# A planner that orders five queues: durations fitted to the trace, and a planned wait of VectorE for GpSimd

## The chip, the core and the metric

The kernel runs on one core of one Trainium2 chip. The metric is the device time of one execution in microseconds (us). Three executions of the kernel before took 3527.23, 3532.02 and 3536.44 us, so the median is 3532.02 us.

A core has engines that work side by side, each through its own queue and strictly in the order of that queue: TensorE (PE in the profile, its weight loads PEld), VectorE (DVE), ScalarE (ACT), GpSimd (POOL) and SyncE (SP), which here issues all DMAs. SBUF is the memory on the chip, PSUM the memory in eight banks that matmuls write. DVE and ACT read PSUM; POOL works on SBUF alone.

## What is computed

Two layers over 128 sequences of 32 tokens and 256 features. Each layer attends to a context of 257 tokens for every sequence, then does self-attention, then a feed-forward block; in the second layer the attention to the context is joined by a gated second attention, and the feed-forward block is eight experts with a router.

```python
x = x + _L0_xattn_ref(_layernorm(x), ctx_2048, ...)        # 16 heads, keys with an RMS norm
x = x + _L0_attn_ref(_layernorm(x), ...)                   # differential attention
x = x + _L0_ffn_ref(_layernorm(x), ...)                    # weights through a 4-bit round trip
x = x + _L1_xattn_ref(_layernorm(x), mask, ctx_2048, ...)  # 32 heads, rotary, gate
x = x + _L1_attn_ref(_layernorm(x), ...)                   # 16 heads, causal
x = x + _L1_ffn_ref(_layernorm(x), ...)                    # 8 experts, top-2 fallback
return x
```

## The kernel before

**Tiling.** Four sequences of 32 tokens make one tile of 128 rows (`h`, 32 tiles). Values are kept as a 16-bit high part and a 16-bit remainder, so that fp32 accuracy comes out of 16-bit matmuls. Nearly every PSUM result therefore is read twice: ACT writes the high part, DVE subtracts it from PSUM and writes the remainder (`split_ps`, lines 381 to 388). For softmax weights ACT writes the exponential `P` and POOL the remainder `Pl` (`expP`, lines 918 to 925).

**Streams.** The work is written as some 30 streams, each a generator: loading and projecting the context (`ctx`), `rowpass` (row maxima of the scores, tiles `mx`, `m16`, `pl`, `mT`), `pvpass` (exponentials and the products with V, tiles `P`, `Pl`, `Uc`), the layer norm `ln_T` (tiles `bmv`, `brs`, `lnh`) ahead of every block, the self-attentions B and E, the feed-forward blocks C and F, and so on. The first layer's streams run until about 1,770 us of the trace, the second layer's after that; streams of one layer overlap freely.

**The planner.** Class `Est` (lines 87 to 223) decides the order. Each instruction is emitted through a wrapper (`Eng`, line 226, with its call in line 234, which is why every line of the profile says L234), and `Est.note` gives it a planned start: not before its operands are there, and then in the first gap of its engine that is long enough (`fit`, line 111), so that a later emitted instruction can be planned into an earlier gap. How long it holds its engine comes from `Est.cost` (line 137), a table of formulas in nanoseconds by engine, operation, element count and place of the operands. `LAT` (line 90) is added until a consumer on another engine may start.

The plan is used twice. `pipeline` (line 355) picks the stream that goes on next by the planned time at which it can. At the end the instructions of each of the five queues PE, ACT, DVE, POOL and DMA are sorted by planned start, and a dependence from each to the next pins that order into the program (lines 376 to 379):

```python
for L in [est.log[k] for k in PIN]:
    L.sort(key=lambda x: x[:2])
    for (_, _, a), (_, _, b) in zip(L, L[1:]):
        self.tc.add_manual_dep(b, a.name, dep, reason="issue order")
```

Planned times never reach the chip: an instruction starts there when its queue comes to it and its semaphores allow. Only the order is the plan's.

Of the kernel before, what the change touches and what calls it, by code (L numbers as in the profile page):

```python
# [17 lines left out]
PSUM = bass.MemoryType.PSUM  # L18
# [66 lines left out]


class Est:
    """Estimates when each instruction can run. It only decides the order in which units of work are emitted."""

    LAT = {"pe": 196.0, "act": 150.0, "dve": 135.0, "pool": 75.0, "dma": 910.0}  # L90

    def __init__(self):
        self.busy = {k: ([], []) for k in ("pe", "act", "dve", "pool", "hw", "dma")}
        self.w, self.r, self.free, self.slots, self.rec = {}, {}, {}, {}, []
        self.end = self.pe = 0.0
        self.cols, self.acc, self.prev, self.first, self.group = {}, {}, {}, {}, {}
        self.log = {k: [] for k in ("pe", "act", "dve", "pool", "dma")}

# [37 lines left out]
    @staticmethod  # L136
    def cost(e, op, outs, ins):
        def n(a):
            return math.prod(a.shape[1:])

        def half(a):
            return mybir.dt.size(a.dtype) == 2 and a.space != PSUM
        o = outs[0]
        if e == "pe":
            if op == "transpose":
                return max(25.0, n(o) / 2.4 * (2 if mybir.dt.size(ins[0].dtype) == 4 else 1))
            return 426.0 if mybir.dt.size(ins[0].dtype) == 4 else max(25.0, n(ins[1]) / 2.4 + 1.0)
        m = max([n(o)] + [n(a) for a in ins])
        if e == "act":
            return (50.0 if ins[0].space == PSUM else 92.0) + 93.0 * (len(ins) > 1) + 0.84 * m  # L150
        if e == "pool":
            return 300.0 + 165.0 * n(o) if n(o) <= 8 else 149.0 + 2.1 * m
        f = 1.0
        if op == "transpose":
            return 602.0
        if all(half(a) for a in [o] + [a for a in ins if n(a) > 1]):
            f = 0.5 if op == "tensor_tensor" else 0.3
        return 68.0 + 1.04 * m * f

    @staticmethod  # L160
    def region(a):
# [17 lines left out]
    def note(self, e, op, outs, ins, inst):  # L179
        t = 0.0  # L180
        R = [(a.tensor.name, self.region(a)) for a in ins]
        Wr = [(a.tensor.name, self.region(a)) for a in outs]
        for w, L in ((False, R), (True, Wr)):
            for n, (p0, p1, lo, hi) in L:
                t = max(t, self.first.get(n, 0.0), self.group.get(n, 0.0) if e == "pe" else 0.0)
                if w:
                    t = max(t, self.free.get(n, 0.0))
                    if n not in self.first:
                        t = max(t, self.first.get(self.prev.get(n), 0.0) + 1.0)
                for (q0, q1, l2, h2, wr), (end, by) in self.acc.get(n, {}).items():  # L190
                    if (w or wr or h2 == PSB) and q0 < p1 and p0 < q1 and l2 < hi and lo < h2:
                        t = max(t, end if (w or h2 == PSB) and by == e and e != "dma" else end + self.LAT[by])
        if e == "dma":
            t = self.fit("hw", t, 500.0)
            st = t - 500.0
            end = self.fit("dma", t + 650.0, math.prod(outs[0].shape) * mybir.dt.size(outs[0].dtype) / 360.0)
        else:
            d = self.cost(e, op, outs, ins)
            if e == "pe" and self.cols.get(int(t / TICK) - 1, 0.0) < WARM:
                d = max(25.0, 2.0 * d - 1.0)  # L200
            end = self.fit(e, t, d)
            st = end - d
            if e == "pe":
                k = int(end / TICK)
                self.cols[k] = self.cols.get(k, 0.0) + math.prod(ins[-1].shape[1:]) * ins[0].shape[0] / 128
                self.pe = max(self.pe, end)
                self.group[Wr[0][0]] = end
        self.log[e].append((st, len(self.log[e]), inst))
        for n, _ in Wr:
            self.first.setdefault(n, st)  # L210
        fin, end = end, end + self.LAT[e]
        for n, k in R:
            A = self.acc.setdefault(n, {})
            k += (False,)
            A[k] = max(A.get(k, (0.0, e)), (fin, e))
            self.r[n] = max(self.r.get(n, 0.0), end)
        for n, (p0, p1, lo, hi) in Wr:
            A = self.acc.setdefault(n, {})
            for k in [k for k in A if p0 <= k[0] and k[1] <= p1 and lo <= k[2] and k[3] <= hi]:
                del A[k]  # L220
            A[p0, p1, lo, hi, True] = (fin, e)
            self.w[n] = max(self.w.get(n, 0.0), end)
        self.end = max(self.end, end)
# [1449 lines left out]
```

## Time and profile before

| | value |
|---|---|
| median of 3 runs | 3532.02 us (3527.23 to 3536.44) |
| profiled execution, first to last instruction | 3532.9 us |
| mean granted TensorE clock | 0.917 of full speed |
| instructions | 95,750 |
| DVE / ACT / POOL instructions | 7,365 / 6,339 / 2,313 |
| HBM traffic | 318.82 MB read, 180.19 MB written, 141 GB/s |

Busy time in two long stretches, one in each layer (us, and share of the stretch):

| stretch | PE | DVE | ACT | POOL | PE clock |
|---|---|---|---|---|---|
| 353 to 1590 (1237 us) | 1104.6 (89%) | 975.5 (79%) | 807.6 (65%) | 821.8 (66%) | 0.97 |
| 1943 to 3356 (1413 us) | 1224.6 (87%) | 1209.4 (86%) | 956.6 (68%) | 782.2 (55%) | 0.90 |

How to read it: the span lies within the spread of the timed runs, so sums made on the trace can be set against the median as they are. A group of instructions is given by engine, operation, what it writes and reads, its shapes, its count, its busy time and the mean of one in ns. The recorded length of an instruction is not quite the time that it holds its engine: on DVE the next instruction often starts some 80 ns before the record of the last ends, on ACT some 100 ns, on POOL some 40 ns.

### The profile page before, as it was taken

The numbers are of one execution on the slowest core, as the hardware profiler recorded it, in microseconds if no ns is written. First come the engines' busy times: TensorE is split into PE (matmuls) and PEld (weight loads), VectorE is DVE, ScalarE is ACT, GpSimd is POOL, SyncE is SP. The second block draws the span as 40 slices with busy tenths as digits, with TensorE's granted clock in tenths as the row PEclk, the third lists the DMA queues.
The fourth block names the chain that finished last, engine by engine and source line by source line (L and its number), as shares of the span: only waits on it lengthen the run. The fifth ranks groups of instructions, "written<-read, shape, count | busy, mean of one in ns | idle before, by whom it ended". The sixth has DMA issues, their size and how long they took to land.

```text
span 3532.9 us, 95750 instructions
## 1 busy us (share of the span) xinstructions
PE 3027.0 (86%) x35473; PEld 2261.8 (64%) x35473; DVE 2868.5 (81%) x7365; ACT 2239.1 (63%) x6339; POOL 2020.9 (57%) x2313
## 2 busy tenths in 40 slices
PE   5889898898888899898776889989888898888888
PEld 2545666666666666665564677767676776766676
DVE  6888787788777887878777888879888888898876
ACT  3446666566666676675567766676676775766672
POOL 2445666666666676675564554555555655555562
PEclk9989999999999999998876899989898998989999
DMA  5646676666677677676546434454454544445420
GB/s 138 194 142 194 178 203 191 188 182 193 195 207 209 193 209 214 180 209 187 129 117 175 109 88 91 113 112 95 105 120 101 119 111 94 99 104 117 107 50 10
DMA packets 685970, 509.90 MB, mean 144 GB/s; under 512 B 226524, under 2 KB 673244, under 8 KB 685500
## 3 DMA queue, kind: packets, MB, share of 16 engines
q1 hardware_dynamic: 685500, 503.77, 54.2%
q8 instruction: 279, 4.57, 0.6%
q14 instruction: 191, 1.56, 0.2%
HBM read 318.82 MB, written 180.19 MB: 141 GB/s over the span
## 4 chain that ended last, share of the span: by engine, by line
DVE 18%; PE 16%; ACT 8%; DMA 5%; issue 2%; SPq 1%; POOL 1%; DVEq 0%; ACTq 0%; POOLq 0%
PE bank L234 16%; DVE mx L234 4%; DMA QstD<-ed 2%; ACT P L234 1%; ACT Uc L234 1%; DVE dS L234 1%; DVE xt L234 1%; SPq L234 1%; DVE eS L234 1%; DVE glu_t L234 1%; DVE fhid L234 1%; DVE lnh L234 1%; DVE rbt L234 1%; ACT Qb L234 1%; DVE s L234 1%
## 5 line engine op out<-in xcount | busy, mean ns | idle before, releaser
L234 POOL TENSOR_TENSOR Pl<-P 128x512 f16<-128x512 f32 x768 | 813.6, 1075 | 317.7 <-ACT P L234 313.5
L234 ACT ACTIVATE P<-bank 128x512 f32<-128x512 f32 x768 | 438.4, 600 | 114.8 <-PE bank L234 94.3
L234 DVE TENSOR_REDUCE mx<-bank 128x2 f32<-128x512 f32 x768 | 479.6, 681 | 7.9 <-PE bank L234 7.9
L234 ACT COPY Uc<-bank 32x68 f32<-32x68 f32 x1536 | 314.7, 205 | 159.9 <-PE bank L234 142.2
L234 ACT CAST vv<-bank 128x256 f16<-128x256 f32 x512 | 200.9, 403 | 251.5 <-DVE vv L234 119.6
L234 PE MATMUL bank<-V,P 128*128 128x68 f16 (+1 forms) x4096 | 304.6, 199 | 26.9 <-ACT P L234 16.6
L234 DVE TENSOR_TENSOR vv<-bank,vv 128x256 f16<-128x256 f32 x512 | 213.1, 423 | 122.9 <-ACT vv L234 115.3
L234 POOL TENSOR_TENSOR fhl<-fhid 128x256 f16<-128x256 f32 x256 | 156.7, 615 | 273.0 <-DVE fhid L234 229.6
L234 PE MATMUL bank<-V,Pl 128*128 128x36 f16 (+1 forms) x3072 | 290.7, 194 | 10.7 <-POOL Pl L234 10.6
L234 PEld LDWEIGHTS <-P 128*128 128x128 bf16 x4096 | 264.8, 102 | 42.4 <-issue 16.7
L234 PEld LDWEIGHTS <-Kst 97*128 97x128 f16 x4096 | 240.5, 102 | 76.2 <-issue 48.2
L234 PEld LDWEIGHTS <-Pl 128*128 128x128 f16 x3072 | 243.7, 100 | 41.9 <-POOL Pl L234 17.4
L234 ACT ACTIVATE glu_t<-bank 128x256 f32<-128x256 f32 x352 | 134.1, 383 | 172.3 <-PE bank L234 138.3
L234 PE MATMUL bank<-QstD,Kst 97*128 97x128 f16 x2048 | 207.0, 233 | 29.6 <-ACT P L234 9.5
L234 PEld LDWEIGHTS <-ch 128*128 128x128 f16 x2048 | 196.3, 100 | 54.8 <-issue 23.4
L234 POOL TENSOR_TENSOR kk<-kb,kk 128x512 f16<-128x512 f32 x128 | 147.1, 1167 | 111.0 <-ACT kk L234 110.8
L234 PEld LDWEIGHTS <-hT 128*128 128x128 f16 x1536 | 138.0, 103 | 113.3 <-issue 34.7
L234 PE MATMUL bank<-khf,eh 32*128 32x256 f16 (+1 forms) x1536 | 153.8, 296 | 56.8 <-DMA khf<-kd 13.7
L234 DVE SCALAR_TENSOR_TENSOR glu_t<-glu_t,bank 128x256 f32<-128x256 f32 x352 | 144.8, 411 | 68.6 <-ACT glu_t L234 67.3
L234 POOL TENSOR_TENSOR cl<-ct,ch 128x1024 f16<-128x1024 f32 x64 | 137.5, 2149 | 34.6 <-DMA xt<-in_x 22.5
L234 POOL TENSOR_TENSOR ss<-ss,sq 128x512 f32<-128x512 f32 (+1 forms) x65 | 82.7, 1272 | 120.9 <-ACT sq L234 72.9
L234 POOL TENSOR_TENSOR rbt<-rbt,rbt 128x512 f32<-128x512 f32 x64 | 83.0, 1297 | 100.9 <-DVE rbt L234 72.1
(470 smaller groups left out, 9459.5 us busy)
## 6 DMA issues: line engine op xcount, KB each, us to landing
Kst<-kd SPq DMA_DIRECT2D x384, 256.0 KB
kd<-kk SPq DMA_DIRECT2D x128, 512.0 KB
vd<-vv SPq DMA_DIRECT2D x256, 136.0 KB
V<-vd SPq DMA_DIRECT2D x64, 544.0 KB
vd<-vv SPq DMA_DIRECT2D x256, 132.0 KB
V<-vd SPq DMA_DIRECT2D x64, 528.0 KB
ct<-in_ctxm SPq DMA_DIRECT2D x64, 512.0 KB
khf<-kd SPq DMA_DIRECT2D x128, 256.0 KB
```

The lines of the kernel that those rows point to most:

```text
L234: r = f(*a, **k)
```

## The change

Only `Est` is touched: no instruction is added or taken away, and no operand, tile or buffer changes. Three things are done.

First, `cost` is rewritten for ACT, POOL and some of DVE. Second, a new function `lock` moves the planned ready time of a DVE instruction to the end of the POOL operation that is planned to run at that moment, if it is a `tensor_scalar`, `tensor_copy`, `tensor_tensor` or `scalar_tensor_tensor` and none of its operands lies in PSUM. Third, `note` keeps the planned spans of POOL in a list `pl` for that purpose.

```diff
         if e == "act":
-            return (50.0 if ins[0].space == PSUM else 92.0) + 93.0 * (len(ins) > 1) + 0.84 * m
+            ps = ins[0].space == PSUM
+            d = (50.0 if ps else 92.0) + (127.0 if ps else 93.0) * (len(ins) > 1) + 0.84 * m
+            return d + 100.0 * (len(outs) > 1) + 112.0 * (o.shape[0] in (32, 64))
         if e == "pool":
-            return 300.0 + 165.0 * n(o) if n(o) <= 8 else 149.0 + 2.1 * m
+            if n(o) <= 8:
+                return 350.0 + 160.0 * n(o)
+            d16 = mybir.dt.size(o.dtype) == 2
+            k = (1.665 if mybir.dt.size(ins[-1].dtype) == 2 and ins[-1].tensor.name == ins[0].tensor.name else 1.9) if d16 else 2.1
+            if any(a.ap[-1][0] == 0 for a in ins):
+                k = 1.68
+            return 147.0 + k * m
         f = 1.0
         if op == "transpose":
             return 602.0
         if all(half(a) for a in [o] + [a for a in ins if n(a) > 1]):
             f = 0.5 if op == "tensor_tensor" else 0.3
-        return 68.0 + 1.04 * m * f
+        if op == "reciprocal":
+            f = 5.0
+        d = 58.0 * (op == "scalar_tensor_tensor" and len(ins) > 2)
+        if op == "tensor_copy" and ins[0].space == PSUM and o.shape[0] < 32:
+            f = 0.5
+        return 68.0 + d + 1.04 * m * f
+
+    def lock(self, t, op, outs, ins):
+        if not self.pl or any(a.space == PSUM for a in outs + ins) or op not in ("tensor_scalar", "tensor_copy", "tensor_tensor", "scalar_tensor_tensor"):
+            return t
+        i = bisect.bisect_right(self.pl, (t, 1e18)) - 1
+        return max(t, self.pl[i][1]) if i >= 0 else t
...
             d = self.cost(e, op, outs, ins)
             if e == "pe" and self.cols.get(int(t / TICK) - 1, 0.0) < WARM:
                 d = max(25.0, 2.0 * d - 1.0)
+            if e == "dve":
+                t = self.lock(t, op, outs, ins)
             end = self.fit(e, t, d)
             st = end - d
+            if e == "pool":
+                bisect.insort(self.pl, (st, end))
+                if len(self.pl) > 4000:
+                    del self.pl[:1000]
```

`m` is the largest element count per row among the operands, `n(o)` that of the output, `o.shape[0]` the number of rows written; `len(ins) > 1` is true for an ACT instruction with a scale or bias column, `len(outs) > 1` for one that also writes a row sum.

More of the change, by code (lines that the diff above doesn't have):

```diff
@@ L95, in __init__ @@
         self.end = self.pe = 0.0
+        self.pl = []
         self.cols, self.acc, self.prev, self.first, self.group = {}, {}, {}, {}, {}
```

## The prediction

> **What bounds the kernel now.** I read the page from the top: busy time, then the slices, then the chain of waits.
>
> ```profile
> PE 3027.0 (86%) x35473; PEld 2261.8 (64%) x35473; DVE 2868.5 (81%) x7365; ACT 2239.1 (63%) x6339; POOL 2020.9 (57%) x2313
> ...
> DVE 18%; PE 16%; ACT 8%; DMA 5%; issue 2%; SPq 1%; POOL 1%; DVEq 0%; ACTq 0%; POOLq 0%
> ```
>
> No engine is full. The reader is to see that PE and DVE are both near 85%, and that the chain (it could be followed through the last 51% of the span) lies on DVE for 18 of its 51 points, on PE for 16, on ACT for 8. The order of the queues decides, and DVE is the engine that is last most often: a us saved on DVE is worth about 18/51 = 0.35 us at the end. I use that factor below; it is a choice, since shares of a chain are not a derivative.
>
> Next I asked whether the DVE's busy time is work. The timeline of DVE over 900 to 912 us:
>
> ```profile
> 903.07 0.16 DVE L234 TENSOR_TENSOR mx<-mx,pl 128x8 f32<-128x8 f32 x1
> 903.31 0.43 DVE L234 TENSOR_TENSOR vv<-bank,vv 128x256 f16<-128x256 f32 x1
> 903.65 0.67 DVE L234 TENSOR_SCALAR m<-mx 128x8 f16<-128x8 f32 x1
> ...
> 909.35 0.15 DVE L234 TENSOR_SCALAR brs<-bmv 128x1 f32<-128x1 f32 x1
> ...
> 910.37 0.70 DVE L234 TENSOR_SCALAR bsm<-bsm,nlam 128x2 f32<-128x2 f32 x1
> ```
>
> and of POOL over the same time:
>
> ```profile
> 902.03 2.27 POOL L234 TENSOR_TENSOR kk<-kb,kk 128x512 f16<-128x512 f32 x2 [4.28 <-ACT kk L234]
> ...
> 908.66 1.27 POOL L234 TENSOR_TENSOR ss<-ss,sq 128x512 f32<-128x512 f32 x1 [2.10 <-ACT sq L234]
> 910.01 1.04 POOL L234 TENSOR_TENSOR sl<-ss 128x512 f16<-128x512 f32 x1
> ```
>
> An eight-element instruction takes 0.67 us and ends at 904.32, POOL's pair ends at 904.30; a two-element one takes 0.70 us and ends at 911.07, POOL's `sl` at 911.05. `vv`, with an operand in PSUM (`bank`), runs through the same POOL work in its usual 0.43. So DVE instructions without a PSUM operand do wait on the chip for POOL, inside their own record. The one-element `brs` does not: 0.15 us in the middle of `ss`.
>
> **How much that wait is.** Groups with shapes kept apart, mean of one in ns, against the median of the same tile's instructions (which is unwaited, as most of a group doesn't wait):
>
> ```profile
> L234 DVE TENSOR_SCALAR lnh<-xt,bmv,brs 128x256 f32<-128x256 f32 x192 | 123.6, 659 | 8.7 <-POOL brs L234 6.9 <-PE bank L234 1.1
> L234 DVE TENSOR_SCALAR eh<-qT,const 128x256 f16<-128x256 f16 x128 | 68.3, 590 | 0.0
> L234 DVE TENSOR_SCALAR m<-mx 128x8 f16<-128x8 f32 x64 | 24.8, 387 | 0.8
> L234 DVE TENSOR_SCALAR brs<-bmv 128x1 f32<-128x1 f32 x128 | 19.1, 150 | 2.7
> ```
>
> `lnh`: 192 x (659 - 414) = 47 us. `eh`: 128 x (590 - 279) = 40. The six narrow groups of the row pass (`mx`, `m`, `pl` at 8 and 16 elements, 64 each; means 400, 348, 387, 374, 372, 291, medians 173, 173, 169): 73. `eS`: 128 x (439 - 285) = 20. `nfmk`: 180 x (395 - 290) = 19. `bS`: 64 x (373 - 280) + 64 x (452 - 352) = 12. `e`: 64 x (463 - 343) = 8. Sum 219; the other narrow groups (`bss`, `bmx`, `aos`, `bsm`, `qn`, the router's) bring some 80. **About 300 us of DVE's 2868 is waiting for POOL**, by the single records in 521 instructions of some 2,120 of this kind, 0.57 us each. By stretch, 132 us lie in 353 to 1590 and 100 us in 1943 to 3356. The plan before knows nothing of it.
>
> **The change, part by part.**
>
> *The planned wait.* The chip waits already; new is only that the plan puts such an instruction behind the POOL operation, so that others, mostly with PSUM operands, are sorted ahead of it. What is queued behind it on DVE no longer waits. Between two ends: nothing is avoided (0 us), or all 300. All can't be: `lock` looks once, before `fit`, so an instruction that a full DVE pushes on can land in the next POOL operation unseen, and 57% of POOL's operations follow the one before within 60 ns, so one that comes late meets a whole new one. None can't be either: whoever waits for POOL's end is let in at once (the two examples end 20 ns after it), also where the next POOL operation stands ready. With nothing nearer to choose by, I take half: 150 us off DVE, x 0.35 = **53 us**.
>
> *ACT's durations.* Three rows against the old formula:
>
> ```profile
> L234 ACT COPY Uc<-bank 32x68 f32<-32x68 f32 x1536 | 314.7, 205 | 159.9 <-PE bank L234 142.2 <-DVE glu_t L234 0.5 <-DVE va L234 0.4
> L234 ACT COPY aT<-bank 64x128 f32<-64x128 f32 x256 | 66.2, 259 | 15.9 <-PE bank L234 11.2 <-DVE m L234 1.1 <-issue 0.8
> L234 ACT ACTIVATE ue<-bank 32x128 f32<-32x128 f32 x256 | 68.2, 266 | 11.2 <-PE bank L234 7.7 <-DVE glu_t L234 0.5
> ```
>
> Before, the plan gave `Uc` 50 + 0.84 x 68 = 107 ns; the row has 205, and in the records the next ACT instruction starts 218 ns later. The new 219 is right, as is 270 for `aT` and `ue` (157 before). Planned ACT time grows by 112 x 2064 = 231 us (16 half-height `glu_t` with them), the row sums (100 x 224) and biases (34 x 128) add 27. After each group of products four `Uc` follow one another, so the plan before held ACT free 0.45 us too early, and put PE's next matmuls where ACT had not emptied a bank. PE's idle time that ACT ended is 43.7 (`P`) + 26.1 (`Uc`) + 9.8 (`aT`) + 9.2 (`hT`) = 89 us. Bounds: 0 to half of it, 45. I take a quarter: **22 us**.
>
> *POOL's durations.* `Pl` was planned at 149 + 2.1 x 512 = 1224 ns, now 999; its row has 1075, and the next POOL operation starts 998 ns after it. 768 x 225 = 173 us less; with `fhl`, `hidl` and `aTl` (416 x 114 = 47), the other wide ones (65) and the narrow powers (12 more), 273 us less. Products with `Pl` move forward in PE's queue. PE's waits that POOL ended are 10.6 (`Pl`) and under 40 in all: bounds -10 to +14, as they can also come too early; taken **4 us**.
>
> *DVE's durations.* Reciprocals, three-operand `scalar_tensor_tensor` (474 ns in the row of `xt<-bank,w,xt` beside 415 without `w`) and `mT` copies. Some 20 us of planned DVE time, an order of magnitude under the waits: nothing, hidden in the choice of one half above.
>
> *What moves with it.* All five queues are sorted anew, SP's 2,999 DMA issues too. A DMA follows its producer; those on which PE waits are `QstD` and `QstA` (34.5 and 29.8 us), fed by `mT` at the end of the row pass. If `m` and `pl` are planned later, that load is later; the row pass has a tile's whole time of slack, so I cost it at nothing, at most 64 us if that cover went.
>
> **A rule against the change.** The Trainium skill (SBUF — State Buffer, Who interferes with whom) says that DVE and GpSimd share a port pair as an exclusive lock, that whoever issues first has it for the whole instruction, and that the other blocks. The plan has one half: POOL never waits. By the rule, 521 DVE instructions of 0.15 to 0.4 us placed at POOL's ends would hold up POOL by some 130 us, 57% busy to 61%. The trace has `Pl` at a mean of 1075 against a median of 1039, 28 us in 768. By either the cost is under 2 us at the end, as POOL holds 1 of 51 points of the chain. The page also excepts instructions with one SBUF input outside the two-port modes: `brs` and `ssq` at one element (150 ns, unwaited) get a planned wait that the chip lacks. At most 160 x 0.57 (POOL's busy share) x 0.57 us = 52 us of planned delay on the layer norm, x 0.35 = 18 us; taken as nothing, since other streams fill DVE there.
>
> **Sum.** 53 + 22 + 4 = 79 us. Against the profiled execution: 3532.9 - 79 = **3454 us**; the median of the runs is 0.9 us away from the span, so it stands for both.
>
> **The rivals.**
> *The waits stay.* `lock` doesn't do what it says, because DVE in the full stretches is pushed past the gap it computed. Speaks for it: DVE at 86% in 1943 to 3356. Against: the waits there are 7% of the stretch, 11% in the looser one. Then ACT and POOL alone remain, and a tenth of the rest: 3532.9 - 22 - 4 - 7 = 3500 us.
> *Slower: the filler blocks.* What is sorted ahead of a waiting instruction is often a remainder such as `vv` or `glu_t`, which itself waits for ACT (115 and 67 us of DVE's idle time, the largest). If it isn't ready on the chip, DVE stands before it while the narrow instruction behind it could have run. The price: one us on half of 521, 260 us, less the 150 saved, = 110 x 0.35 = 39 us: 3572 us. It decides where the filler's mean wait is above the 0.57 us that it replaces; today such fillers wait 0.24 us each (`vv`: 123/512), which speaks against.
> *Nothing comes of it.* DVE's wait turns into planned idleness and PE at 89% has no more to give: 3533 us.
>
> **How the numbers follow.** Forecast 0.55 (3390 to 3510, with 75 to 240 us of waits avoided), waits stay 0.12, nothing 0.09, slower 0.24. About 0.3%, 10.6 us, can be told from no change; the first two lie wholly beyond it. So faster 0.67, same 0.09, slower 0.24. The lower end is everything: 300 x 0.35 + 45 + 14 = 164 us, 3370; the upper end reaches the slower case, 3570.
>
> **What would show it.** DVE's busy time should fall to about 2720 with the same 7,365 instructions; the means of `lnh` and `eh` should fall by half the way to 414 and 279; PE's idle time ended by ACT `P` and `Uc` should fall below 60 us. `Pl` should stay near 1075. If DVE's busy time falls and the span doesn't, the factor 0.35 is wrong; if it stays, `lock` fails; if idle time before `vv` and `glu_t` grows past 300 us in sum, the filler blocks.

## The result, and the profile after

The changed kernel took 3551.37 us (median of 4 runs, 3547.77 to 3562.16) against 3530.57 us for the kernel before on the same chip. The quotient of these medians is 1.0059; the ratio that goes with the 95% interval of 1.0047 to 1.0085, and is used below, is 1.0066: slower by 0.7%, where 79 us less had been forecast. The profiled execution spans 3550.8 us.

The page of the changed kernel, its busy times, the clock and the chain of waits:

```profile
PE 3051.8 (86%) x35473; PEld 2274.1 (64%) x35473; DVE 2868.3 (81%) x7365; ACT 2238.2 (63%) x6339; POOL 2021.4 (57%) x2313
...
PEclk9999999999999999997876898888988899888889
...
PE 38%; DVE 32%; DMA 11%; ACT 8%; issue 6%; POOL 3%; SPq 2%; DVEq 0%; ACTq 0%; POOLq 0%
```

The clock row of the kernel before:

```profile
PEclk9989999999999999998876899989898998989999
```

The chain now covers the whole span, where that of before could be followed through 51% of it; DVE has 32 of 100 points, close to the 18 of 51 behind the factor 0.35.

DVE, ACT and POOL are busy to within 1 us of what they were (2868.5, 2239.1 and 2020.9). Only PE is longer, by 25 us, for the same 35,473 matmuls, at a mean granted clock of 0.903 instead of 0.917. PE's idle time even fell, from 506 to 499 us. So the 18 us by which this profiled execution is longer stand, on PE, in the length of its matmuls; which feature of the order lowers the clock is not shown.

As DVE is as busy as before, nothing of its waiting went away. Its groups with shapes kept apart (busy us, mean ns, then idle time before):

```profile
L260 DVE TENSOR_SCALAR lnh<-xt,bmv,brs 128x256 f32<-128x256 f32 x192 | 122.2, 651 | 19.7 <-POOL brs L260 17.1 <-PE bank L260 0.9
L260 DVE TENSOR_SCALAR eh<-qT,const 128x256 f16<-128x256 f16 x128 | 61.8, 526 | 0.0
L260 DVE TENSOR_TENSOR eS<-eS,emx 128x128 f32<-128x128 f32 x128 | 63.1, 547 | 0.4
L260 DVE TENSOR_SCALAR m<-mx 128x8 f16<-128x8 f32 x64 | 17.9, 279 | 0.4
```

`m` at eight elements fell from 387 to 279 ns, `lnh` from 659 only to 651, and `eS` rose from 439 to 547. Counted in the single records of both traces in one way (length above the tile's short instructions), DVE waited 298 us for POOL before and 305 after, in 521 and 529 instructions. The planned wait moved the waits about and removed none.

What moved is where work lies. The context's last projection was stored at 1587 us of the trace instead of 1639, but the first layer's last store came at 1852 instead of 1844, and the second layer took 1696 us instead of 1686.

### The profile page after: what moved, and what is told of

It reads as the page before. It is cut to its first block, busy times and chain, and to the rows that moved or that the text cites. A ratio compares the mean times of both kernels' runs of the same rounds, so it can differ in the third digit from the quotient of the medians.

```text
span 3550.8 us, 95780 instructions
## 1 busy us (share of the span) xinstructions
PE 3051.8 (86%) x35473; PEld 2274.1 (64%) x35473; DVE 2868.3 (81%) x7365; ACT 2238.2 (63%) x6339; POOL 2021.4 (57%) x2313
## 4 chain that ended last, share of the span: by engine, by line
PE 38%; DVE 32%; DMA 11%; ACT 8%; issue 6%; POOL 3%; SPq 2%; DVEq 0%; ACTq 0%; POOLq 0%
PE bank L260 38%; DVE mx L260 7%; SPq L260 2%; DMA QstA<-e2d 2%; DVE vv L260 1%; DVE lnh L260 1%; DVE eS L260 1%; DMA QstD<-ed 1%; ACT P L260 1%; DVE glu_t L260 1%; DVE rbt L260 1%; DVE dS L260 1%; DVE xt L260 1%; DVE eh L260 1%; DVE fhid L260 1%
## 5 line engine op out<-in xcount | busy, mean ns | idle before, releaser
L260 POOL TENSOR_TENSOR Pl<-P 128x512 f16<-128x512 f32 x768 | 804.5, 1063 | 350.0 <-ACT P L260 343.4
L260 PE MATMUL bank<-V,P 128*128 128x68 f16 (+1 forms) x4096 | 311.9, 200 | 27.7 <-ACT P L260 11.0
L260 PE MATMUL bank<-V,Pl 128*128 128x36 f16 (+1 forms) x3072 | 295.8, 195 | 20.7 <-POOL Pl L260 19.6
L260 DVE TENSOR_TENSOR vv<-bank,vv 128x256 f16<-128x256 f32 x512 | 212.1, 423 | 93.3 <-ACT vv L260 88.0
L260 PE MATMUL bank<-khf,eh 32*128 32x256 f16 (+1 forms) x1536 | 171.3, 307 | 53.8 <-DVE fhid L260 9.6
L260 DVE SCALAR_TENSOR_TENSOR glu_t<-glu_t,bank 128x256 f32<-128x256 f32 x352 | 144.4, 410 | 67.6 <-ACT glu_t L260 66.1
```

The costliest lines, as they stand in the source:

```text
L260: r = f(*a, **k)
```

## The experiments

All ratios below are against the kernel before, timed on the same chip between the runs. "Second layer" is the time from the first layer's last store to 3 us before the end of the span, in the profiled execution. No kernel changes the arithmetic. They differ in the order of their queues and in one thing more, which the section on the change denies: the plan has a third use. `tk` (line 330) takes the PSUM bank that is free first in planned time, so banks change with the plan. `bank0` takes 4,473 of PE's outputs in the plan of before, 4,726 in that of the changed kernel, and 4,717 in that of before with one latency 1 ns longer. What the banks alone do to the time was not tried.

### The change taken apart

**Durations alone.** The two lines that call `lock` are taken out of the changed kernel.

```diff
-            if e == "dve":
-                t = self.lock(t, op, outs, ins)
```

> The new durations without the planned wait. Theory A (the planned wait is what costs: it moves DVE work late in the plan for a wait that the chip has anyway): this is faster than before, about 3505 us, and the last projection of the context still ends near 1590 us as in the changed kernel. Theory B (the new durations draw the first layer's context work forward and leave the passage between the layers thin): about 3550 us, context ended near 1590, first layer's last store near 1850. Theory C (any re-sorting lands within about 1% of before, with no sign of its own): anywhere from 3500 to 3565, and not the sum of its parts. In all three DVE's waits for POOL stay near 300 us.

Measured: 3554.02 us, ratio 1.0044 (1.0030 to 1.0058), context ended at 1644 us, DVE's waits 298 us. Theory A, that the planned wait is what costs, falls: without it the kernel is as slow. Theory B gave the time, but its cause is absent: the context isn't drawn forward here.

**The planned wait alone.** `cost` is that of before, `lock` is kept.

```diff
-            ps = ins[0].space == PSUM
...
+            return (50.0 if ins[0].space == PSUM else 92.0) + 93.0 * (len(ins) > 1) + 0.84 * m
```

> The planned wait with the durations of before. Theory A: slower than before, 3555 to 3575 us. Theory B: near before, 3520 to 3540, context ended near 1640 us. Theory C: anywhere from 3500 to 3565. If the planned wait works at all, the chip's waits of DVE for POOL fall well under 300 us (POOL's longer durations here make the plan's waits longer, so they would be over-avoided); if the plan's places don't carry over to the chip they stay at 280 to 310.

Measured: 3621.58 us, ratio 1.0237 (1.0222 to 1.0253), outside every range given; waits 295 us. Taken as they stand, the parts cost 0.44% and 2.37% and their union 0.66%. The parts don't add, as theory C has it; its range of 3500 to 3565 us failed here all the same.

**ACT's durations alone**, in the kernel before.

```diff
-            return (50.0 if ins[0].space == PSUM else 92.0) + 93.0 * (len(ins) > 1) + 0.84 * m
+            ps = ins[0].space == PSUM
+            d = (50.0 if ps else 92.0) + (127.0 if ps else 93.0) * (len(ins) > 1) + 0.84 * m
+            return d + 100.0 * (len(outs) > 1) + 112.0 * (o.shape[0] in (32, 64))
```

> Only ACT's durations are those of the trace. My prediction's term: 22 us less than before, 3510, with PE's idle time ended by ACT P and Uc under 60 us. Theory B: context ended earlier than 1639 us, total not faster. Theory C: 3500 to 3565.

Measured: 3568.33 us, ratio 1.0093 (1.0076 to 1.0110), just above the 3565 that theory C allowed. A truer model of one engine gave a slower kernel. At the place itself the forecast came true (see the part on the prediction below).

**The planned wait made to hold.** In the changed kernel, the wait is repeated until the gap that is found lies outside every POOL operation planned so far.

```diff
-            if e == "dve":
-                t = self.lock(t, op, outs, ins)
+            while e == "dve":
+                s0 = self.find(e, t, d)
+                t1 = self.lock(s0, op, outs, ins)
+                if t1 <= s0:
+                    break
+                t = t1
             end = self.fit(e, t, d)
```

(`find` is the search of `fit` without its booking.)

> The changed kernel, but the planned wait is repeated until the place that the gap search gives lies outside every POOL operation planned so far. If the wait fails because it looks once, ahead of the gap search, DVE's waits for POOL fall from 305 us to under 180 and DVE's busy time from 2868 to about 2740 us; with 0.35 us at the end for each, 3551 - 45 = about 3505 us. If it fails because the plan's places aren't the chip's, the waits stay above 270 and the time within 1% of the changed kernel.

Measured: 3556.02 us, ratio 1.0051 (1.0034 to 1.0067). The page's busy times of this kernel:

```profile
PE 3049.4 (86%) x35473; PEld 2275.7 (64%) x35473; DVE 2818.0 (79%) x7365; ACT 2243.4 (63%) x6339; POOL 2023.9 (57%) x2313
```

and two of its DVE groups:

```profile
L274 DVE TENSOR_SCALAR lnh<-xt,bmv,brs 128x256 f32<-128x256 f32 x192 | 107.6, 575 | 22.8 <-POOL brs L274 19.2 <-PE bank L274 1.7
L274 DVE TENSOR_SCALAR m<-mx 128x8 f16<-128x8 f32 x64 | 16.3, 255 | 0.8
```

This lies between the two expectations. Looking once was part of the failure: DVE's busy time falls by 50 us and the waits from 305 to 242 us, in 427 instructions. But four fifths of the waits stay, and the time at the end stays too.

Where the plan itself puts these instructions shows why. The planner can be run again from each kernel, and its 7,365 DVE instructions in planned order have, one by one, the names of those in the trace. So each of the 2,133 instructions that `lock` handles can be followed from its planned place to its wait on the chip (a wait is here a record over 50 ns longer than its tile's median; this gives 306 us for the changed kernel, and 240 for the repeated wait). Each entry is the number of instructions, then their waits on the chip:

| planned start of the DVE instruction | durations alone | changed kernel | repeated wait |
|---|---|---|---|
| inside a POOL operation planned before it | 757, 173 us | 343, 96 us | 0 |
| inside a POOL operation planned after it | 450, 95 us | 519, 127 us | 697, 160 us |
| at the end of a POOL operation | 0 | 283, 50 us | 303, 52 us |
| elsewhere | 926, 29 us | 988, 34 us | 1,133, 29 us |

In the changed plan 862 of the 2,133 still start inside a POOL operation, and theirs are 223 of the 306 us. For 343 the gap search went on into one after `lock` had looked. For the other 519 `lock` could see nothing: the POOL operation was planned only later, over a DVE instruction that already stood there. The repeated wait clears the first kind and leaves the second. The planned places do carry over: of the 862, 43% wait on the chip, of those planned elsewhere 5%. But a place at the end of a POOL operation is little better than one inside: 107 of the 283, 38%, wait.

How DVE and POOL meet on the chip is seen in the changed kernel's timeline. DVE over 2437 to 2441 us (start, length, instruction, and xN for N of them merged):

```profile
2437.55 3.45 DVE L260 TENSOR_TENSOR eS<-eS,emx 128x128 f32<-128x128 f32 x4
```

and POOL over 2436 to 2442 us:

```profile
2436.53 4.13 POOL L260 TENSOR_TENSOR Pl<-P 128x512 f16<-128x512 f32 x4 [1.03 <-ACT P L260]
```

Four subtractions take 3.45 us, beside four `Pl` that take 4.13; alone, such a subtraction has a record of 0.28 us (the tile's median before is 285 ns), and the next starts 0.2 us after it. In the single records the second `Pl` begins at 2437.523 and the first `eS` at 2437.555; the third at 2438.521 and the second `eS` at 2438.633; the fourth at 2439.571 and the third `eS` at 2439.677. Each time POOL's next operation has started 0.03 to 0.11 us before the subtraction, which takes 1.12 to 1.15 us beside it. The last subtraction, with no `Pl` left, takes 0.28. In the plan the first of the four stands just before a `Pl` and the other three, pushed on because DVE is taken, stand inside that `Pl`: `lock` had looked at the moment when they were ready. Of the waiting instructions, 297 of 521 before and 291 of 529 after began within 0.25 us of a POOL operation's start, so the planned wait did not change this pattern either.

### How much a re-sorting moves by itself

If the parts don't add, the order may matter more than what made it. So the kernel before was built again with one planned latency 1 ns longer, which makes the model neither better nor worse. For PE it reads as follows; the other three change 150 to 151, 135 to 136 and 75 to 76.

```diff
-    LAT = {"pe": 196.0, "act": 150.0, "dve": 135.0, "pool": 75.0, "dma": 910.0}
+    LAT = {"pe": 197.0, "act": 150.0, "dve": 135.0, "pool": 75.0, "dma": 910.0}
```

> The kernel before with 1 ns more latency after PE in the plan (197 instead of 196): no better and no worse as a model, only other ties and gaps. Theory C (each order is a draw; before is a good one): 3535 to 3620, most likely near 3560, that is as slow as the changed kernel and its parts. Theory D (a change this small keeps the time, so that the losses of the changed kernel and its parts come from what they do): within 0.3% of before, 3526 to 3547.

> The kernel before with 1 ns more latency after ACT in the plan (151 instead of 150). Theory C: 3535 to 3620, near 3560. Theory D: 3526 to 3547.

> The kernel before with 1 ns more latency after DVE in the plan (136 instead of 135). Theory C: 3535 to 3620, near 3560. Theory D: 3526 to 3547.

> The kernel before with 1 ns more latency after POOL in the plan (76 instead of 75). Theory C: 3535 to 3620, near 3560. Theory D: 3526 to 3547. Over the four: by theory C they spread by 1% or more and their mean lies above before.

| 1 ns after | time, us | ratio (95%) | second layer, us |
|---|---|---|---|
| PE | 3586.65 | 1.0163 (1.0132 to 1.0194) | 1737 |
| ACT | 3569.29 | 1.0113 (1.0087 to 1.0139) | 1716 |
| DVE | 3580.69 | 1.0141 (1.0116 to 1.0167) | 1746 |
| POOL | 3579.58 | 1.0140 (1.0113 to 1.0168) | 1744 |

Theory D is refuted four times. One nanosecond costs over 1%, about twice what the whole change cost. Theory C was right about the sign and less so about the spread: the four lie within 0.5% of each other, around a mean ratio of 1.0139, and before stands alone below them. Its second layer, 1686 us, is 30 to 60 us shorter than any of theirs; its first layer (1844 us) is like theirs (1831 to 1848). On PE it differs from them in both respects: it is busy 3027.0 us (theirs 3047.0 to 3064.6) at a clock of 0.917 (theirs 0.902 to 0.911), and idle 506 us (theirs 514 to 531). Among near-identical plans the kernel before is a good draw. Whether by luck is not shown: a kernel that had been kept for being fast would look the same. Why its order is better was not tried, nor were neighbours with a shorter latency.

Then the same was done with the changed kernel (the same edit in its `LAT` line).

> The changed kernel with 1 ns more latency after PE in the plan. The four of before lay at 3569 to 3587, mean 3579. Theory E (the change does improve the typical order, by the tens of us that were forecast, and lost only against the lucky draw that before is): the four of the changed kernel average 3500 to 3560. Theory F (the change gives the typical order nothing; 3551 is a lucky draw of its own): they average 3570 to 3590.

> The changed kernel with 1 ns more latency after ACT in the plan. Theory E: 3500 to 3560 on average over the four. Theory F: 3570 to 3590.

> The changed kernel with 1 ns more latency after DVE in the plan. Theory E: 3500 to 3560 on average over the four. Theory F: 3570 to 3590.

> The changed kernel with 1 ns more latency after POOL in the plan. Theory E: 3500 to 3560 on average over the four. Theory F: 3570 to 3590. By both, DVE's waits for POOL stay at 280 to 320 us in each.

| 1 ns after | time, us | ratio (95%) | second layer, us | DVE's waits for POOL, us |
|---|---|---|---|---|
| PE | 3493.73 | 0.9894 (0.9873 to 0.9915) | 1683 | 291 |
| ACT | 3517.18 | 0.9969 (0.9959 to 0.9978) | 1676 | 310 |
| DVE | 3488.89 | 0.9887 (0.9867 to 0.9906) | 1685 | 298 |
| POOL | 3573.22 | 1.0128 (1.0105 to 1.0152) | 1687 | 312 |

Theory E held: they average 3518 us. Against the neighbours of before the mean ratio is 0.9970 to 1.0139, 1.7% less, with a standard error of about 0.6% from the spread of the draws (0.0112 and 0.0021, four each). With both originals counted in, five draws each, it is 0.9989 to 1.0111, 1.2% less. So the typical order of the changed planner is probably shorter, by some 43 to 60 us, and the two kernels of this study compare a good draw of the old planner with a poor one of the new. With so few draws a 95% interval reaches from nothing to twice that, so the whole time alone does not settle it. Three of the neighbours beat both kernels; the best takes 3488.89 us.

The gain is clearer in the second layer, where all five of the changed planner's orders take 1676 to 1696 us and the four neighbours of before 1716 to 1746. With the 1686 us of before itself counted in, the means of five are 1685 and 1726 us, 40 us apart with a 95% interval of 10 to 71. Busy times over the second layer of one neighbour of before (1 ns after DVE), columns PE, PEld, DVE, ACT, POOL with counts, then granted clock, DMA share and GB/s:

```profile
1831.00:3578.00 1747.00, 1474.29 (x18754) 1168.44 (x18750) 1437.38 (x3744) 1132.05 (x3253) 907.52 (x1160) 0.88 0.42 99
```

and of the best neighbour of the changed kernel:

```profile
1804.00:3489.00 1685.00, 1444.65 (x18448) 1150.13 (x18447) 1407.52 (x3700) 1110.52 (x3191) 893.84 (x1142) 0.88 0.42 100
```

In the neighbour of before PE is idle 273 us there, in that of the changed kernel 240, and the latter's PE is busy 30 us less, with 306 fewer matmuls in the stretch (at 1474.29/18754, 79 ns each, 24 of the 30 us). So the second layer is shorter partly because a little of its work was done before it began, and partly because PE stood still less. It is not fewer waits of DVE: these are 291 to 312 us in the four, as in the kernel before.

### Which part brings it

Neighbours of the kernels with one part each, by the same three edits, fill the table. The wait alone and the durations alone have three neighbours each; in the table their rows, and that of both, count the original kernel in (first ratio), and the row of before does not.

> The new durations without the planned wait, with 1 ns more latency after PE in the plan. So far the time from the first layer's last store to the end is 1717 to 1747 us in the four neighbours of before, and 1676 to 1696 in the changed kernel and its four. Theory G (the durations alone bring the gain): 1675 to 1700 here, whole time 3490 to 3560. Theory H (the planned wait is needed too): 1705 to 1730, whole time 3540 to 3570.

> The new durations without the planned wait, 1 ns more latency after ACT. Theory G: 1675 to 1700 us for the second layer. Theory H: 1705 to 1730.

> The new durations without the planned wait, 1 ns more latency after DVE. Theory G: 1675 to 1700 us for the second layer. Theory H: 1705 to 1730.

> The planned wait with the durations of before, 1 ns more latency after PE. lock_only itself took 1755 us in the second layer and 3622 in all. Theory G: the wait gives nothing by itself, 1715 to 1760 us for the second layer, 3560 to 3625 in all. Theory H, in the form that the wait alone brings half of the gain: 1690 to 1715, 3530 to 3560 in all.

> The planned wait with the durations of before, 1 ns more latency after ACT. Theory G: 1715 to 1760 us for the second layer, 3560 to 3625 in all. Theory H: 1690 to 1715, 3530 to 3560.

> The planned wait with the durations of before, 1 ns more latency after DVE. Theory G: 1715 to 1760 us for the second layer, 3560 to 3625 in all. Theory H: 1690 to 1715, 3530 to 3560.

| plan | ratios | mean | second layer, us |
|---|---|---|---|
| as before (neighbours) | 1.0163, 1.0113, 1.0141, 1.0140 | 1.0139 | 1716 to 1746 |
| durations alone | 1.0044, 1.0055, 1.0091, 1.0136 | 1.0082 | 1710 to 1722 |
| wait alone | 1.0237, 1.0034, 1.0106, 1.0049 | 1.0107 | 1702 to 1754 |
| both | 1.0066, 0.9894, 0.9969, 0.9887, 1.0128 | 0.9989 | 1676 to 1696 |

(The neighbours' times: durations alone 3559.58, 3573.72 and 3592.18 us after PE, ACT and DVE; wait alone 3551.49, 3579.06 and 3558.95.) Theory G is wrong: the durations alone leave the second layer at 1710 to 1722. Of theory H, the band for the second layer with the durations held in all three neighbours, while the form that the wait alone brings half failed in two of three (1729 and 1726). Neither part makes the second layer as short as both do. In the whole time, one part alone gains 0.3 to 0.6% over the neighbours of before, which a standard deviation of up to 0.9% among four draws does not separate from nothing. Why the two need each other was only argued: `lock` waits for POOL's planned end, which without the new durations lies 225 ns too late for each `Pl`. It stays open.

## Why the prediction was wrong, point by point

**DVE's 300 us of waiting for POOL** were sized rightly: 298 us before, 305 after, and in the other orders about as much, but for the 242 of the repeated wait.

**"I take half: 150 us off DVE" is the term that failed.** Measured: none; DVE's busy time stayed at 2868.3 us, which the prediction had given as the sign that `lock` fails. The step assumed that an instruction for which `lock` waits is planned outside POOL's operations. In the changed plan 862 of 2,133 still start inside one, with 223 of the 306 us of waits. The prediction had named one reason, the single look ahead of the gap search (343 instructions, 96 us), but only to exclude all 300. The larger one it did not have: POOL operations that are planned later over a DVE instruction already placed (519, 127 us). It excluded zero with "whoever waits for POOL's end is let in at once"; of the 283 that the plan puts at such an end, 107 wait all the same, 50 us in sum. The repeated wait removed 63 us, and that is the most that any planned wait in this study removed. The rival "the waits stay" describes what DVE did, and its reason, the pushing on, is part of it; its 3500 us failed.

**The factor 0.35** was not confirmed: 63 us fewer waits went with 3556 us instead of 3551. It is not refuted either, for 63 x 0.35 = 22 us is far less than the 84 us between the fastest and the slowest of five orders of the changed kernel.

**ACT's 22 us** came at the place and not at the end. PE's waits (us in total, times, longest) for ACT's `P` and `Uc`, in the kernel before:

```profile
PE bank L234 <- ACT P L234: 43.7, 60, 2.8
PE bank L234 <- ACT Uc L234: 26.1, 44, 1.6
```

in the changed kernel:

```profile
PE bank L260 <- ACT P L260: 36.8, 44, 7.6
PE bank L260 <- ACT Uc L260: 26.1, 23, 3.3
```

and with ACT's durations alone:

```profile
PE bank L236 <- ACT P L236: 23.8, 38, 2.2
PE bank L236 <- ACT Uc L236: 18.6, 30, 2.0
```

The change brings 69.8 to 62.9 us, 7 less and not below 60. ACT's durations alone bring 42.4, 27 less, the size that was forecast; yet that kernel has a ratio of 1.0093. It is one draw, 0.5% below the mean of the neighbours of before, less than can be told. So what shrank at the place was not seen at the end, and the quarter that was taken is neither confirmed nor refuted.

**POOL's 4 us** were not tried by themselves; at the place they have the other sign, as PE's wait for `Pl` rose from 10.6 to 19.6 us in the changed kernel.

**What was costed at nothing** held for POOL: `Pl` has a mean of 1063 ns after 1075, so the wait was not shifted to POOL. It held for the loads too: PE's waits for `QstD` and `QstA` are 64.3 us before and 66.1 after. They were not read rightly, though: nearly all are for the parts loaded from `ed` and `e2d`, and only 1.2 us before for those from `mT`. The filler that blocks, the rival for a slower kernel, is refuted: DVE's idle time before `vv` fell from 122.9 to 93.3 us, and before `glu_t` from 68.6 to 67.6. The slower result has another cause, the next point.

**What no step had.** The sum began at 3532.9 us as if that were what the old plan gives. It is 1.4%, about 49 us, below what plans next to it give. For the typical order the forecast of a better planner was probably right in its sign (43 to 60 us shorter, 79 forecast), but that is luck: the way that it named, fewer waits of DVE, was not taken. For the one order that was measured it was wrong. The range should have carried a term for the draw. The trace of before could not show its size; only neighbours can.

## What to carry to other kernels

- Where a planner fixes the order of several queues, one kernel is one draw. Before a change of its model is judged, or a good time is believed, build a few neighbours that differ by a nanosecond: here a neighbour was up to 2.0% from its original (the wait alone, 1.0237 and 1.0034), where the change was 0.7%, and the best one found was 1.1% faster than the kernel before.
- A busy engine may be waiting inside its own records. Compare a group's mean with its median, and with its twin that has no part in the contention, before counting busy time as work.
- Read out where the plan puts the instructions before the chip is asked whether they wait. A rule that looks once, at what is planned so far, left 862 of 2,133 where they were not to be.

## What the runs showed of the hardware

- DVE and POOL can take turns in step: three subtractions, each 0.28 us alone, took 1.12 to 1.15 us, each beside one `Pl`, and a fourth with no `Pl` beside it took 0.28. The three `Pl` took 1.04 to 1.09 us, against a median of 1.04 before, so nearly all of the waiting fell on DVE.
- A one-element `tensor_scalar` takes hardly any part: of the 128 such `brs`, with POOL busy 57% of the time, none took over 0.2 us before and one after, and the means are 150 and 145 ns.
- The same 35,473 matmuls were busy between 3019.4 us (1 ns after PE, changed kernel, granted clock 0.919) and 3067.9 us (1 ns after POOL, changed kernel, clock 0.898). More idle time of PE does not by itself explain the lower clock: the kernel before idles 506 us at 0.917, the changed kernel 499 us at 0.903.
